# Products of zeros between the transposes of a recurrent stage

## The chip, the cores and the metric

The kernel runs on one core of one Trainium2 chip. Its metric is the device time of one execution in microseconds. Before the change three runs took 1701.95, 1700.95 and 1701.09 us, a median of 1701.09.

The engines are named as in the profile: PE is TensorE (PEld its weight loads), DVE is VectorE, ACT is ScalarE, POOL is GpSimd, SP is the engine that issues the large transfers.

## What is computed

A sequence of up to 50 items for each of B = 1024 users is turned into a spike rate, and each rate is multiplied with the whole table of N = 100001 embeddings of 128 numbers:

```
emb = emb_table.at[0].set(0.0)
e = emb[seq]
prefix = jnp.cumsum(e, axis=1)
denom = jnp.minimum(t_idx[None, :], lengths[:, None]).astype(e.dtype)
uF = prefix / denom[:, :, None]
mean = uF.mean(axis=0)
var = uF.var(axis=0)
y = (uF - mean) * lax.rsqrt(var + BN_EPS) * gamma + beta
...
def step(v, x):
    v = v + (x - v) / TAU
    spike = atan_spike(v - V_TH)
    v = v - lax.stop_gradient(spike) * V_TH
    return (v, spike)
...
uF_out = spikes.mean(axis=0)
scores = uF_out @ emb.T
```

The result has 1024 x 100001 numbers, 409.6 MB.

## The kernel before, in words

The work has two stages. The first walks through the T = 50 steps of the sequence, with the 128 features on the partitions and the 1024 users along the free dimension, in two halves of 512 (one bank of PSUM each). The second multiplies the spike counts with the table, chunk by chunk, and stores the scores. The order of each engine's instructions is the order of the program, nothing is moved by a scheduler; waits are put in where a buffer or a value is needed.

A step t of the first stage (lines 270 to 346) goes as follows.

- POOL gathers the rows of step t + 1 from the table (`gather`, line 185): eight indirect transfers of 128 rows each into one of three buffers `e`. A buffer is free again when the transposes of its earlier step have read it.
- PE transposes the eight blocks of `e` and adds each onto the running sum in PSUM, `pre[0]` or `pre[1]` (line 282). Each of the eight waits for its own gather.
- DVE divides each half by the count of items (line 291, into `uF`) and takes its statistics (line 292). It needs the four transposes of that half.
- PE then adds the correction of the next step to `pre` (`correct`, line 242): it takes away what table row 0 has added, by a product over 50 rows.
- DVE merges the statistics (line 296), ACT takes the root (line 300) and shifts `uF` (line 303), DVE finds the spikes of the step before (`spike`, line 262).
- PE adds those spikes to the counts (`counted`, line 252): a bf16 product with the identity, 512 columns, one for each half, into two more banks of PSUM, `count[0]` and `count[1]`.
- DVE ends the inverse root (lines 314 to 320), ACT makes the input (line 328), DVE the membrane voltage (lines 336, 331).
- In steps 42, 44 and 46 a piece of the table is prepared for the second stage as well: eight transposes on PE (line 101), a copy on ACT (line 130), a subtraction on DVE (line 134).

On PE the order is therefore: transposes of step t, corrections of step t + 1, counts of step t - 1, transposes of step t + 1.

The first seven chunks of the table are fetched at the start of the program; the next are fetched in the second stage, in which each of the counts is multiplied with two parts of the table (`product`, line 146) and the result is scaled out of PSUM by DVE (line 409) and ACT (line 411) and stored.

Of the kernel before, what the change touches and what calls it, by code (L numbers as in the profile page):

```python
# [13 lines left out]
BF16 = mybir.dt.bfloat16  # L14
# [6 lines left out]
P = 128  # L21
# [6 lines left out]
BANK = 512  # L28
# [3 lines left out]
def rec_kernel(  # L32
# [9 lines left out]
    nc = tc.nc  # L42
    B, T = seq.shape
# [92 lines left out]
    def prepare(c, q, pt):  # L136
        turned(c, q, pt)
        upper(c, q, pt)
        lower(c, q, pt)
# [18 lines left out]
    with ExitStack() as ph:  # L158
        row0p = ph.enter_context(tc.tile_pool(name="rows0", bufs=1))
        once = ph.enter_context(tc.tile_pool(name="once", bufs=1))  # L160
# [21 lines left out]
        def gather(t):  # L182
            es[t] = gp.tile([P, B], F32, tag="e", name=f"e_{t}")
            for n in range(NB):
                nc.gpsimd.indirect_dma_start(  # L185
                    out=es[t][:, n * P : (n + 1) * P],
                    out_offset=None,
                    in_=table,
                    in_offset=bass.IndirectOffsetOnAxis(ap=idx[:, n, t : t + 1].bitcast(U32), axis=0),
                )  # L190
# [41 lines left out]
        count = [accp.tile([P, BANK], F32, tag=f"count{h}", name=f"count{h}") for h in range(B // BANK)]  # L232

        def only(t):

            l = sp.tile([T, D], F32, tag="l", name=f"l_{t}")
            nc.scalar.activation(l, r0n, AF.Copy, scale=ident[:T, t : t + 1])
            return l

        def correct(t, l):  # L240
            for h in range(B // BANK):
                nc.tensor.matmul(  # L242
                    pre[h],
                    lhsT=l,
                    rhs=zT[:, h * BANK : (h + 1) * BANK],
                    start=t == 0,
                    stop=False,
                    skip_group_check=True,
                )

        def counted(t, s, h):
            nc.tensor.matmul(
                count[h],
                lhsT=ident_h,
                rhs=s[:, h * BANK : (h + 1) * BANK],
                start=t == 0,
                stop=t == T - 1,
                skip_group_check=True,
            )

        def spike(s, v, cs):
            nc.vector.tensor_single_scalar(s[:, cs], v[:, cs], V_TH, ALU.is_ge)  # L262

# [6 lines left out]
        for t in range(T):  # L270
            last = t == T - 1
            if t + 1 < T:
                gather(t + 1)
            e = es.pop(t)
            if last:
                spike(s, v, whole)
                nc.vector.tensor_tensor(negv, s, v, ALU.subtract)
            uF = up.tile([P, B], F32, tag="uF", name=f"uF_{t}")
            bs = sp.tile([P, B // BANK, 6], F32, tag="bs", name=f"bs_{t}")
            for h, cs in enumerate(halves):  # L280
                for k in range(0, BANK, P):
                    nc.tensor.matmul(  # L282
                        pre[h][:, k : k + P],
                        lhsT=e[:, h * BANK + k : h * BANK + k + P],
                        rhs=ident,
                        start=False,
                        stop=last,
                        is_transpose=True,
                        skip_group_check=True,
                    )  # L290
                nc.vector.scalar_tensor_tensor(uF[:, cs], rlen[:, cs], 1.0 / (t + 1), pre[h], ALU.max, ALU.mult)  # L291
                nc.vector.bn_stats(bs[:, h, :], uF[:, cs])  # L292
            if not last:
                correct(t + 1, l)
            mv = sp.tile([P, 2], F32, tag="mv", name=f"mv_{t}")
            nc.vector.bn_aggr(mv, bs.rearrange("p h s -> p (h s)"))  # L296


            r = sp.tile([P, 1], F32, tag="r", name=f"r_{t}")
            nc.scalar.activation(r, mv[:, 1:2], AF.Sqrt, bias=eps)  # L300
            nm = sp.tile([P, 1], F32, tag="nm", name=f"nm_{t}")
            nc.vector.tensor_scalar_mul(nm, mv[:, 0:1], -1.0)
            nc.scalar.activation(uF, uF, AF.Identity, bias=nm)
            ve = sp.tile([P, 1], F32, tag="ve", name=f"ve_{t}")
            nc.vector.tensor_scalar_add(ve, mv[:, 1:2], BN_EPS)


            if t:
                if not last:
                    spike(s, v, whole)  # L310
                for h in range(len(halves)):
                    counted(t - 1, s, h)

            nc.vector.reciprocal(r, r)
            q = sp.tile([P, 1], F32, tag="q", name=f"q_{t}")
            nc.vector.tensor_mul(q, r, r)
            nc.vector.scalar_tensor_tensor(q, q, -0.5, ve, ALU.mult, ALU.mult)
            nc.vector.scalar_tensor_tensor(r, q, 1.5, r, ALU.add, ALU.mult)
            a = sp.tile([P, 1], F32, tag="a", name=f"a_{t}")
            nc.vector.tensor_scalar(a, r, hgb[:, 0:1], None, ALU.mult)  # L320

            vt = vp.tile([P, B], F32, tag=f"v{t % 2}", name=f"v_{t}")
            st = lp.tile([P, B], BF16, tag="s", name=f"s_{t}")

            def x(cs):
                nc.scalar.activation(vt[:, cs], uF[:, cs], AF.Identity, bias=hgb[:, 1:2], scale=a)  # L328

            def step(cs):  # L330
                nc.vector.scalar_tensor_tensor(vt[:, cs], negv[:, cs], -0.5, vt[:, cs], ALU.mult, ALU.add)  # L331

            if not last:
                x(whole)
                if t:
                    nc.vector.tensor_tensor(negv, s, v, ALU.subtract)  # L336
                step(whole)
                v, s = vt, st
                if t + 2 < T:
                    l = only(t + 2)  # L340

                if T - 8 <= t < T - 2 and t % 2 == 0:
                    q = (t - T + 8) // 2
                    prepare(0, q, vp.tile([P, HALF], F32, tag="v1", name=f"pt_{q}"))
# [7 lines left out]
        for h, cs in enumerate(halves):  # L352
            step(cs)
            spike(st, vt, cs)
            if h == 0:
                counted(T - 1, st, 0)
                nc.scalar.copy(countA, count[0][:, :P])
# [84 lines left out]
```

## Time and profile before

| | us |
|---|---|
| median of 3 runs | 1701.09 |
| lowest, highest | 1700.95, 1701.95 |
| profiled execution, its own time | 1702.82 |
| its span, first to last instruction | 1701.1 |

| part of the span | PE busy | DVE busy | ACT busy | POOL busy | granted clock of PE | DMA share |
|---|---|---|---|---|---|---|
| 0 to 64 | 27.96 | 21.33 | 11.24 | 41.41 | 0.59 | 0.76 |
| 64 to 504 | 242.80 | 279.40 | 110.56 | 291.68 | 0.55 | 0.16 |
| 504 to 597 | 58.91 | 70.42 | 28.57 | 45.26 | 0.56 | 0.12 |
| 597 to 1701 | 876.69 | 576.76 | 481.06 | 0.00 | 0.93 | 0.98 |

The first three rows are the first stage: the start, in which the table's first chunks come in; the steps; and the last steps, in which the second stage is prepared. The fourth row is the second stage. All columns but the last two are microseconds. The granted clock is the share of the full TensorE clock that the throttle gave, the DMA share the mean busy share of the core's 16 DMA engines. A busy PE is not a PE at its peak: the records of its products overlap, and their ends are modelled. What ended a wait is inferred from semaphores; "remote" stands where no instruction of the profile is found for it.

### The profile page before, as it was taken

What the parts mean: (1) busy time and instruction counts of PE and PEld (TensorE: products, weight loads), DVE (VectorE), ACT (ScalarE), POOL (GpSimd) and SP (SyncE); (2) the same over time, 40 slices, a digit from 0 to 9 for tenths busy, and PEclk for the clock granted to TensorE, in tenths of its full rate; (3) what the DMA queues carried; (4) which work ended last, traced back from release to release, by engine and by line L of the source; (5) the groups of instructions that cost most, each with busy time, mean ns of one, the idle gap of its engine ahead of it and who ended that gap; (6) DMA issues with size and microseconds to landing.
All of it is one profiled execution on the core that took longest, in us unless ns stands there. A gap on an engine that the chain in (4) does not pass through costs nothing.

```text
span 1701.1 us, 13009 instructions
## 1 busy us (share of the span) xinstructions
PE 1206.4 (71%) x4621; PEld 844.5 (50%) x4634; DVE 947.9 (56%) x1257; ACT 631.4 (37%) x698; POOL 378.4 (22%) x406
## 2 busy tenths in 40 slices
PE   5445554565456597877777887777777778888886
PEld 2122222222223376666555665655655556666664
DVE  3556665676567774554455555554454555556553
ACT  2222222222222354444444444444444444445442
POOL 7666666666666200000000000000000000000000
PEclk6555555555555598999999999899999999999998
DMA  9211111111111089999999999999999999999998
GB/s 348 95 45 45 47 48 47 43 48 48 47 44 47 22 344 408 424 422 409 410 401 407 401 407 402 405 410 411 402 402 406 401 400 397 425 416 415 419 415 346
DMA packets 58329, 488.12 MB, mean 287 GB/s; under 512 B 12485, under 2 KB 13208, under 8 KB 33688
## 3 DMA queue, kind: packets, MB, share of 16 engines
q1 hardware_dynamic: 45464, 461.06, 66.1%
q0 software_dynamic: 12800, 26.24, 5.3%
q8 instruction: 36, 0.59, 0.1%
q14 instruction: 29, 0.24, 0.0%
HBM read 77.65 MB, written 409.60 MB: 286 GB/s over the span
## 4 chain that ended last, share of the span: by engine, by line
DMA 43%; DVE 22%; PE 15%; another core or an unknown queue 10%; ACT 6%; issue 3%; POOL 0%; SPq 0%; ACTq 0%; DVEq 0%; POOLq 0%
DMA scores<-o 42%; PE po L146 14%; ACT o L411 4%; DVE bs L292 4%; DVE uF L291 4%; DVE v L331 3%; DVE s L262 3%; DVE negv L336 2%; DVE o L409 2%; ACT v L328 1%; DMA e<-in_L_rec_emb_table,idx 1%; DVE mv L296 1%; PE pt L101 1%; DVE a L320 1%
## 5 line engine op out<-in xcount | busy, mean ns | idle before, releaser
L409 DVE TENSOR_SCALAR o<-po 128x1024 f32<-128x1024 f32 x390 | 463.1, 1220 | 473.9 <-DMA scores<-o 351.9
L411 ACT ACTIVATE o<-po 128x1024 f32<-128x1024 f32 (+1 forms) x390 | 385.1, 1018 | 573.0 <-DMA scores<-o 376.1
L146 PE MATMUL po<-hi,countC 128*128 128x512 f32 x784 | 343.1, 438 | 155.0 <-ACT o L411 154.9
L185 POOL DMA_INDIRECT e<-in_L_rec_emb_table,idx x400 | 377.7, 944 | 190.4 <-issue 109.4
L242 PE MATMUL pre<-zT,l 50*128 50x512 f32 x200 | 183.8, 1065 | 233.1 <-DVE uF L291 221.6
L146 PE MATMUL po<-lo,countC 128*128 128x512 f32 x784 | 327.0, 418 | 0.0
L146 PEld LDWEIGHTS po<-hi,countC 128*128 128x128 f32 x784 | 162.1, 207 | 215.2 <-ACT o L411 182.4
L146 PE MATMUL po<-hi,countB 128*128 128x512 f32 x588 | 234.7, 399 | 22.1 <-ACT o L411 22.1
L146 PE MATMUL po<-lo,countB 128*128 128x512 f32 x588 | 229.6, 391 | 0.0
L242 PEld LDWEIGHTS pre<-zT,l 50*128 50x128 f32 x200 | 54.0, 301 | 305.7 <-issue 265.5
L146 PEld LDWEIGHTS po<-lo,countC 128*128 128x128 f32 x784 | 162.3, 207 | 31.9
L291 DVE SCALAR_TENSOR_TENSOR uF<-rlen,pre 128x512 f32<-128x512 f32 x100 | 67.8, 678 | 185.3 <-remote 172.0
L300 ACT ACTIVATE r<-mv,eps 128x1 f32<-128x1 f32 x50 | 14.7, 295 | 384.0 <-DVE mv L296 280.7
L134 DVE TENSOR_TENSOR lo<-pt,hi 128x1024 fp32r<-128x1024 f32 x98 | 117.3, 1217 | 50.6 <-ACT hi L130 45.8
L101 PE MATMUL pt<-ident,rows 128*128 128x128 f32 x782 | 107.5, 282 | 44.6 <-ACT o L411 39.3
L146 PEld LDWEIGHTS po<-hi,countB 128*128 128x128 f32 x588 | 110.9, 189 | 54.3 <-ACT o L411 32.2
L101 PEld LDWEIGHTS pt<-ident,rows 128*128 128x128 f32 x782 | 90.3, 144 | 73.1 <-ACT o L411 58.1
L146 PEld LDWEIGHTS po<-lo,countB 128*128 128x128 f32 x588 | 111.1, 189 | 21.8
L130 ACT CAST hi<-pt 128x1024 fp32r<-128x1024 f32 x98 | 99.0, 1011 | 45.3 <-PE pt L101 40.3
L282 PE MATMUL pre<-ident,e 128*128 128x128 f32 x400 | 99.5, 423 | 14.0 <-DMA e<-in_L_rec_emb_table,idx 10.4
L282 PEld LDWEIGHTS pre<-ident,e 128*128 128x128 f32 x400 | 86.2, 228 | 39.4 <-issue 23.9
L328 ACT ACTIVATE v<-uF,hgb,a 128x1024 f32<-128x1024 f32 (+1 forms) x51 | 60.8, 1192 | 49.1 <-DVE a L320 24.8
(58 smaller groups left out, 701.6 us busy)
## 6 DMA issues: line engine op xcount, KB each, us to landing
scores<-o SPq DMA_DIRECT2D x190, 2048.0 KB
rows<-in_L_rec_emb_table SPq DMA_DIRECT2D x24, 2048.0 KB
scores<-o SPq DMA_DIRECT2D x8, 848.5 KB
e<-in_L_rec_emb_table,idx POOLq DMA_INDIRECT x400
scores<-o SPq DMA_DIRECT2D x2, 1024.0 KB
scores<-o SPq DMA_DIRECT2D x3, 512.0 KB
scores<-o SPq DMA_DIRECT2D x2, 256.0 KB
rows<-in_L_rec_emb_table SPq DMA_DIRECT2D x1, 512.0 KB
```

The lines of the kernel that those rows point to most:

```text
L101: nc.tensor.transpose(pt[:, k0 : k0 + kw], rows[c][:kw, q * KQ + k0 // P, :], ident[:kw, :kw])
L130: nc.scalar.copy(vh, vp)
L134: nc.vector.tensor_tensor(vl, vp, vh.bitcast(F32), ALU.subtract)
L146: nc.tensor.matmul(po[:, :kw], lhsT=counts[n], rhs=part[:, k0 : k0 + kw], start=j == 0, stop=j == 1,)
L185: nc.gpsimd.indirect_dma_start(out=es[t][:, n * P : (n + 1) * P], out_offset=None, in_=table, in_offset=bass.IndirectOffsetOnAxis(ap=idx[: ...
L242: nc.tensor.matmul(pre[h], lhsT=l, rhs=zT[:, h * BANK : (h + 1) * BANK], start=t == 0, stop=False, skip_group_check=True,)
L282: nc.tensor.matmul(pre[h][:, k : k + P], lhsT=e[:, h * BANK + k : h * BANK + k + P], rhs=ident, start=False, stop=last, is_transpose=True, ...
L291: nc.vector.scalar_tensor_tensor(uF[:, cs], rlen[:, cs], 1.0 / (t + 1), pre[h], ALU.max, ALU.mult)
L292: nc.vector.bn_stats(bs[:, h, :], uF[:, cs])
L328: nc.scalar.activation(vt[:, cs], uF[:, cs], AF.Identity, bias=hgb[:, 1:2], scale=a)
L409: nc.vector.tensor_scalar_mul(o[:, h0 : h0 + hw], po[:, :hw], 1.0 / T)
L411: nc.scalar.mul(o[:, h0 : h0 + hw], po[:, :hw], 1.0 / T)
```

## The change

A tile of zeros is made once on DVE. From step 2 on, PE adds three products of that tile with itself to the counts behind each of a step's transposes but the last. A product has 128 rows, 128 columns of weights and 512 moving columns in bf16, as one of the counts has; the three go to `count[0]`, `count[1]` and `count[0]` again. They add zero, so the counts keep their values. There are seven such places in a step, 21 products in each of the steps 2 to 49, and 1008 in all; each comes with a load of its weights. Nothing else moves: the order on the other engines is the same, but for the one clearing on DVE ahead of the first step.

```diff
+        zero = once.tile([P, BANK], BF16, tag="zero", name="zero")
+        nc.vector.memset(zero, 0.0)
+
+        def idle():
+            for h in (0, 1, 0):
+                nc.tensor.matmul(
+                    count[h],
+                    lhsT=zero[:, :P],
+                    rhs=zero,
+                    start=False,
+                    stop=False,
+                    skip_group_check=True,
+                )
...
                         is_transpose=True,
                         skip_group_check=True,
                     )
+                    if 1 < t and h * BANK + k + P < B:
+                        idle()
                 nc.vector.scalar_tensor_tensor(uF[:, cs], rlen[:, cs], 1.0 / (t + 1), pre[h], ALU.max, ALU.mult)
```

## The prediction

> **What bounds the kernel now.** I read the slices first, then busy time by stage, then one stretch of the first stage in order of time, then the granted clock around that stretch.
>
> ```profile
> PE   5445554565456597877777887777777778888886
> POOL 7666666666666200000000000000000000000000
> PEclk6555555555555598999999999899999999999998
> DMA  9211111111111089999999999999999999999998
> ```
>
> A slice is 42.5 us. Thirteen of them are the first stage: POOL gathers, TensorE is granted half its clock, the DMA engines are nearly idle. After 597 us the stage of the products follows, with the DMA engines at 0.98, and nothing of the change reaches into it. So the change is worth what it does before 597 us. Busy time of the engines in stretches that run from one restart of POOL's gathers to the next (columns PE, PEld, DVE, ACT, POOL, clock, DMA share, GB/s):
>
> ```profile
> 4.08:60.69 56.61, 25.44 (x56) 11.15 (x56) 17.75 (x40) 8.62 (x12) 38.02 (x41) 0.57 0.82 306
> 60.69:94.72 34.03, 16.05 (x39) 7.97 (x40) 20.67 (x44) 8.61 (x12) 22.64 (x24) 0.55 0.16 47
> 197.31:231.46 34.15, 19.05 (x41) 8.96 (x42) 21.88 (x46) 8.61 (x12) 22.64 (x24) 0.55 0.16 46
> 504.22:527.04 22.82, 14.56 (x36) 7.75 (x38) 16.59 (x34) 6.75 (x9) 15.09 (x17) 0.57 0.16 46
> 527.04:549.75 22.71, 15.88 (x38) 7.64 (x37) 16.40 (x33) 6.75 (x9) 15.09 (x16) 0.58 0.16 47
> ```
>
> The reader is to see one number in all five. 40 gathers in 56.61 us, 24 in 34.03 and 34.15, 16 in 22.82 and 22.71 are each 1.415 to 1.426 us a gather, in runs of five, three and two steps, under heavy DMA traffic (306 GB/s) and light. POOL issues a gather every 1.25 us, though, as the order of time shows:
>
> ```profile
> 217.28 0.94 POOL L185 DMA_INDIRECT e<-in_L_rec_emb_table,idx  x1 [0.30 <-PE pre L242]
> 217.73 1.92 PE L282 MATMUL pre<-ident,e 128*128 128x128 f32 x8
> 218.53 0.94 POOL L185 DMA_INDIRECT e<-in_L_rec_emb_table,idx  x1 [0.31 <-issue]
> ...
> 226.02 0.94 POOL L185 DMA_INDIRECT e<-in_L_rec_emb_table,idx  x1 [0.30 <-issue]
> 231.09 0.69 DVE L291 SCALAR_TENSOR_TENSOR uF<-rlen,pre 128x512 f32<-128x512 f32 x1 [10.81 <-remote]
> 231.46 0.94 POOL L185 DMA_INDIRECT e<-in_L_rec_emb_table,idx  x1 [4.50 <-remote]
> 231.93 3.75 PE L242 MATMUL pre<-zT,l 50*128 50x512 f32 x4 [12.28 <-DVE uF L291]
> ```
>
> Transposes start at 202.29, 210.01 and 217.73, a step every 7.72 us. VectorE gets the third step's sum not at 219.7, where the transposes end, but at 231.09, 4.1 us after POOL has run out of buffers; POOL waits for the same thing. So three steps take 34.1 us, 11.4 each. I read this as a pace of 1.42 us a gather that POOL's rows do not show and that comes out as a stall in every third step. The trace has no row for the cause ("remote"), so this is a reading and not a sight. The clock in windows of 3.4 us (the two numbers ahead of DMA's GB/s are clock and DMA share):
>
> ```profile
> 213.15:216.55 3.40, 3.33 (x4) 1.12 (x4) 3.30 (x7) 1.16 (x2) 2.49 (x4) 0.50 0.18 49
> 216.56:219.96 3.40, 3.08 (x11) 1.87 (x10) 3.05 (x8) 1.70 (x3) 2.48 (x4) 0.50 0.16 46
> 219.98:223.37 3.39, 0.00 (x0) 0.00 (x0) 0.30 (x1) 0.00 (x0) 2.63 (x3) 1.00 0.21 60
> 650.06:653.45 3.39, 1.09 (x5) 0.56 (x3) 0.00 (x0) 0.00 (x0) 0.00 (x0) 1.00 1.05 443
> 735.39:738.78 3.39, 1.72 (x11) 1.19 (x10) 1.56 (x2) 1.58 (x2) 0.00 (x0) 1.00 1.06 423
> 738.80:742.20 3.40, 3.40 (x20) 2.86 (x19) 2.00 (x2) 1.35 (x2) 0.00 (x0) 1.00 1.01 424
> ```
>
> A window filled by the 50-row corrections (213 to 216) does not raise the clock. One three quarters full of counts and transposes does, and the idle one behind it takes it back. At full clock a window half busy keeps it (735, next still 1.00), a nearly empty one (650) loses it.
>
> [...] here 216.56 to 219.96 holds little but 0.85 us of counts and 1.7 us of transposes and raises it[...]. [...] The trace has two counts in 1.03 us with 0.609 for the last, 0.42 a product, and 0.23 for the stage-two products at full clock.
>
> **The change part by part.** One clearing of a tile on VectorE, before the first step: nothing. In steps 2 to 49, behind seven of the eight transposes, three products of 512 columns: 21 a step, 1008 in all. They wait for nothing, but the transposes behind them wait for them, so a step's *transpose phase* grows. It was 8 x 0.213 (1.91 us with 0.42 for the last) and becomes 8 x 0.213 + 21 x 0.427 = 10.7 us at half clock, and 8 x 0.107 + 21 x 0.216 = 5.4 at full (0.107 as half of 0.213; the stage-two transposes take 1.06 for eight). Behind the last transpose hang VectorE's second half (L291), the correction, the count, the next phase, and POOL, whose next gathers write the buffer that the transposes read. From L291's second half to the count is 3.18 us (213.72 to 216.90), from count to transposes 0.83 (half) or 0.43. With 0.3 for the hand-over the loop is 5.4 + 0.3 + 3.2 + 0.4 = 9.3 us at full clock, 15.0 at half, for 7.7 now. VectorE's own work hides under it.
>
> One group of three steps, in us behind the stalled L291 (231.09 is zero):
> - Before: gathers from 0.4, count 4.5, transposes 5.3 to 7.3.
> - After, first phase: PE has sat idle, so the clock is half at 5.3. The first window three quarters busy ends 2.6 to 6.0 us behind the count at 4.5; I take 4.3, so the clock rises at 8.8. By then 3.5 us of 10.7 are done, the other 7.2 take 3.6: end 12.4 (11.5 to 13.2).
> - POOL's second eight want to start at 10.4 and need that phase's end: 12.7. At 1.42 the first eight are through at 11.8, so the gathers lose 12.7 - 11.8, and the rest of the hand-over: 1.3 us (0 to 2.1).
> - Second phase 16.3 to 21.7, third 25.6 to 31.0. If the clock falls in the pauses of 3.5 us between (corrections and count, a window that the trace leaves open), each ends 1.7 later, the third at 34.7. Gathers 9 to 24 take 16 x 1.42 = 22.7 from 12.7: 35.4. So the third phase stays hidden, barely, and a group costs 1.3 us.
>
> Sum: 13 groups (60.69 to 504.22) x 1.3 = 17. Three pairs with eight transposes more in the second step, whose phase starts only near 20.5 and ends near 26 against 22.7 now: 3 x 3.4 = 10. Steps 48 and 49, which no gather paces, 2 x 2.5 (1.6 at full clock, 3.3 mixed) = 5. Step 2 lies under the stall of 35 to 56 us: nothing. Together +32 us on the profiled execution's 1702.8, so 1735; the median of the runs shown is 1.7 lower, so **1733**.
>
> **The rivals.**
> - *The stall goes* (faster). If the pile of "remote" waits comes from eight transposes in one burst and not from the gathers, spreading them removes it. Then POOL's 1.25 us sets the pace: 400 x 1.25 + 4 = 504 for the end of the gathers, at 569.4 now: -65, +5 for the tail, so 1643; with the clock going up and down, steps of 10.5 to 11 and some 1665 to 1685. For it: no data is missing at 219. Against it: the same 1.42 in five stretches, with transposes spread by waits in the first of them. It decides if a stretch of 24 gathers falls under 34 us.
> - *Hidden*. The clock rises at once in each group, the 1.3 and 3.4 vanish, and the tail is left: +3, 1704 on the median at most.
> - *The clock does not rise* (the change doesn't do what it says): products of zeros count as little as 50 rows do. The loop is 15.0: from step 3's transposes at 64.4, 46 loops end at 754 against 583.9 for step 49's now, +170: 1873. For it: the unraised window of 213. Against: those rows are 50 of 128, these 128. With the clock up half the time, 1780 to 1830.
>
> **How the numbers follow.** Main case 0.62, within 1710 to 1770 (groups from 0.3 to 3 us by the bounds of the first phase and of falling clocks). Clock low 0.10, of which 0.04 under 1800. Hidden 0.12. Stall gone 0.16, of which a quarter is above 1685. The range 1685 to 1800 holds 0.62 + 0.04 + 0.12 + 0.04 = 0.82; the main case's own is 1710 to 1770. Two tenths of a per cent are 3.4 us, about what these runs can tell. Faster takes the stall's 0.16 and a little of Hidden, 0.17; within takes most of Hidden, 0.11; slower 0.72.
>
> **What would show it.** Granted clock in 64 to 504 us: some 0.8 if the step is right, 0.55 if zeros do not count, 0.95 if Hidden is. Transpose phases of 7 us in a group's first step and of 5.4 to 7 in the others. 24 gathers in 35 to 36 us, with POOL waiting for PE ahead of the second eight. L291's "remote" wait shrinks from 10.8 us to a few, because the third phase fills it: it is not time gained. It would be wrong if those waits vanished and the stretch fell toward 30 us, or if the clock fell inside every phase, which takes groups over 38.

## The result and the profile after

The changed kernel takes 1730.20 us (median of 4 runs, 1729.96 to 1730.57), the kernel before 1701.28 (4 runs). The ratio is 1.017, 95% interval 1.0152 to 1.0187. The profiled execution took 1730.02 us, its span 1728.2. The page's slices, 43.2 us each:

```profile
PE   6587887878887887888878777777777788888886
POOL 7566666666665400000000000000000000000000
PEclk7688888888887789999999998998999999999998
DMA  9211111111111139999999999999999999999998
```

The change does what it says: the granted clock is at 0.6 to 0.8 in the first stage, and PE is busy there. Yet the gathers (POOL) reach a little farther to the right. The windows of the stages (PE, PEld, DVE, ACT and POOL busy, clock, DMA share, GB/s):

```profile
64.00:504.00 440.00, 362.07 (x1285) 167.22 (x1310) 277.00 (x563) 107.68 (x151) 282.49 (x299) 0.83 0.16 45
504.00:597.00 93.00, 75.08 (x274) 36.75 (x277) 56.88 (x111) 23.12 (x31) 54.89 (x59) 0.80 0.15 42
597.00:1728.00 1131.00, 901.25 (x3976) 701.42 (x3976) 598.68 (x539) 489.68 (x502) 0.00 (x0) 0.93 0.96 395
```

The clock of 64 to 504 went from 0.55 to 0.83, PE's busy time there from 242.8 to 362.1 us, and POOL did less in it (282 for 292). The merged statistics of step 49, the end of the first stage, come at 621.67 us instead of 591.69, 30.0 later; what follows is 2.9 us shorter. So all of the loss lies in the first stage: 4.7 us up to step 3, 10.0 in steps 4 to 41 (11.76 us each, 11.50 before), 15.2 in the last eight.

Who made POOL and VectorE wait (total us, times, longest), first before, then after:

```profile
DVE uF L291 <- remote: 172.0, 19, 20.6
POOL e L185 <- remote: 64.3, 16, 4.5
POOL e L185 <- PE pre L242: 7.9, 5, 6.7
```

```profile
DVE uF L309 <- PE pre L298: 87.9, 47, 3.5
DVE uF L309 <- remote: 64.1, 8, 24.3
POOL e L185 <- PE pre L298: 45.7, 20, 6.4
POOL e L185 <- PE pre L242: 31.4, 17, 2.0
POOL e L185 <- remote: 26.8, 8, 6.4
```

(Line 309 is line 291 of the kernel before, 298 is 282.) VectorE's "remote" wait fell by 108 us, and no time was gained by it: its waits ahead of this line, whatever ended them, went from 185 to 209 us together, and POOL now waits 104 us instead of 72, 77 of them for PE, in 37 waits and not once in a group. The regular groups of three steps are gone. Times of a typical stretch, read from the starts of the transposes and of the statistics in the trace:

| step | transpose phase, first to last start | mean clock in it | last transpose to second half's statistics | step |
|---|---|---|---|---|
| 16 | 5.30 | 1.00 | 3.47 | 11.56 |
| 17 | 6.95 | 0.76 | 1.52 | 11.65 |
| 18 | 6.25 | 0.85 | 2.25 | 11.68 |
| 19 | 5.29 | 1.00 | 1.89 | 9.98 |
| 20 | 5.30 | 1.00 | 6.01 | 14.10 |
| 21 | 7.07 | 0.75 | 1.03 | 11.41 |

Two things are in it. In some steps part of the phase runs at half clock, and in some VectorE gets its sum late (1.03 us is what it needs). The experiments take them apart.

### The profile page after: what moved, and what is told of

Same layout as the page of the kernel before. It is cut to its first block, busy times and chain, and to the rows that moved or that the text cites. A ratio compares the mean times of both kernels' runs of the same rounds, so it can differ in the third digit from the quotient of the medians.

```text
span 1728.2 us, 15006 instructions
## 1 busy us (share of the span) xinstructions
PE 1368.8 (79%) x5609; PEld 918.9 (53%) x5642; DVE 953.8 (55%) x1258; ACT 631.7 (37%) x698; POOL 379.0 (22%) x406
## 4 chain that ended last, share of the span: by engine, by line
DMA 42%; PE 35%; DVE 11%; ACT 5%; another core or an unknown queue 4%; issue 2%; POOL 1%; SPq 0%; ACTq 0%; DVEq 0%; POOLq 0%
DMA scores<-o 41%; PE po L146 14%; PE count L268 13%; ACT o L429 5%; PE pre L298 4%; DVE s L278 3%; DVE uF L309 2%; DVE bs L310 2%; PE pre L242 2%; PE count L252 2%; DVE o L427 2%; POOL e L185 1%; PE pt L101 1%; DVE v L349 1%
## 5 line engine op out<-in xcount | busy, mean ns | idle before, releaser
L268 PE MATMUL count<-zero 128*128 128x512 bf16 x988 | 305.3, 433 | 1.3 <-issue 0.4
L242 PE MATMUL pre<-zT,l 50*128 50x512 f32 x200 | 124.7, 726 | 65.6 <-DVE uF L309 65.5
L268 PEld LDWEIGHTS <-zero 128*128 128x128 bf16 x1008 | 111.4, 111 | 96.7 <-issue 40.0
L298 PE MATMUL pre<-ident,e 128*128 128x128 f32 x400 | 124.1, 312 | 10.2 <-DMA e<-in_L_rec_emb_table,idx 7.1
L298 PEld LDWEIGHTS pre<-ident,e 128*128 128x128 f32 x400 | 65.0, 163 | 74.3 <-issue 30.3
```

The source lines that it names most:

```text
L242: nc.tensor.matmul(pre[h], lhsT=l, rhs=zT[:, h * BANK : (h + 1) * BANK], start=t == 0, stop=False, skip_group_check=True,)
L268: nc.tensor.matmul(count[h], lhsT=zero[:, :P], rhs=zero, start=False, stop=False, skip_group_check=True,)
L298: nc.tensor.matmul(pre[h][:, k : k + P], lhsT=e[:, h * BANK + k : h * BANK + k + P], rhs=ident, start=False, stop=last, is_transpose=True, ...
```

## Experiments

The runs fell on five chips, and these differ: beside our runs the kernel before took 1702.5 and 1699.6 us on two of them, 1619.1, 1618.8 and 1619.1 on three. The chip of the prediction is of the first kind, *with the stall*. Every run is set against the kernel before on its own chip. The runs under 1, 2 and 3 are one execution each.

Theories at the start, with the letters that expectations use: A, the reading on record, that the gathers have a pace of 1.42 us each which shows as a stall; B, that the stall comes from PE's side, by the pile of transposes; and, from the third run on, "late rows", that the gathered rows come later than recorded, against C, that the completions of PE's work reach the other engines late while POOL gathers.

**1. No gathers (chip with the stall).** SP copies other rows of the table as they lie, so that the sums are those of other rows; once in the kernel before and once in the changed kernel.

```diff
-                nc.gpsimd.indirect_dma_start(
+                nc.sync.dma_start(
...
-                    out_offset=None,
-                    in_=table,
-                    in_offset=bass.IndirectOffsetOnAxis(ap=idx[:, n, t : t + 1].bitcast(U32), axis=0),
+                    in_=table[(t * NB + n) * P : (t * NB + n + 1) * P, :],
```

> The kernel before, with the indirect gathers replaced by plain transfers of table rows from the SP queue (other rows are summed, so the scores differ; bytes and transposes are the same). Theory A, the gathers carry a pace of 1.42 us each and that is the stall: no stall in any step, 7.72 us a step from about 60 us on, last merged statistics near 435 instead of 592, whole about 1545 us. Theory B, the stall belongs to PE and comes with every 24 transposes: still 34 us for three steps, about 1700 us.

> The kernel after with the same replacement (other rows are summed). It shows PE's loop with the added products alone. Theory A: no stalls and no waits of POOL, steps of 9.3 us where the clock is full and up to 11 where it falls in the pauses, mean 10 to 10.5, last merged statistics near 62 + 47 x 10.3 = 546, whole about 1655 us; so the added products cost some 110 us against plain_rows, where the gathers hid all but 29. Theory B: about 1730, as after.

Measured 1545.71 us without products: from step 2 to step 42 the steps take 7.72 us (one takes 8.00), the clock is mostly half (0.829 in the mean of the whole execution), no sum is late. With products 1662.28: steps of 9.12, 10.81 and 10.79 us in turn, 10.24 in the mean. So the stall is there with POOL's gathers and not without them (1702.52 and 1545.71 us; B falls), and the products alone cost 117 us where the gathers hide nothing. The loop of 9.12 us at full clock is the 9.3 of the prediction. But the clock does not stay full in all steps.

**2. Gathers that nobody reads (chip with the stall).** The transposes of the kernel before read one fixed tile; the gathers are issued as ever. (The lines that load this tile once, at the start, are left out here.)

```diff
...
-            e = es.pop(t)
+            e = fixed
+            es.pop(t)
```

> The kernel before, with all gathers issued as before but every step's transposes reading one tile of fixed rows (other rows are summed); nothing on PE depends on a gather any more, and POOL never waits for PE. If the third step is late because its rows are late: no stalls, 7.72 us a step, and the gathers end at their own pace, 4 + 400 x 1.42 = 572 us under theory A, 504 us if 1.25 us is their true pace; the second stage's first buffers wait for them, so about 1680 us or 1615 us. If PE's completions are reported late while gathers pile up (theory C): VectorE still waits about 11 us or more for sums whose transposes are recorded as done.

Measured 1963.09 us, a step of 39.20 us as long as POOL gathers and of 7.72 once it has ended. A step of it in order of time, the gathers left out (they go on at 1.25 us):

```profile
126.76 1.91 PE L285 MATMUL pre<-ident,fixed 128*128 128x128 f32 x8 [0.22 <-issue]
...
150.87 0.69 DVE L294 SCALAR_TENSOR_TENSOR uF<-rlen,pre 128x512 f32<-128x512 f32 x1 [21.49 <-remote]
...
162.06 0.69 DVE L294 SCALAR_TENSOR_TENSOR uF<-rlen,pre 128x512 f32<-128x512 f32 x1 [9.78 <-remote]
```

Eight transposes are recorded from 126.76 to 128.67. VectorE, which waits for nothing else, gets the first four at 150.87 and the other four at 162.06. Late rows are excluded: these rows lay there from the start. What is measured fits C: POOL, which never waits for PE here, issues a gather every 1.25 us without a pause, and every step has such waits, 39.20 us apart. In the other direction nothing is late: VectorE's spikes end at 165.11 in the same step, and PE's counts, which wait for them, start at 165.16. So a PE row's end in this trace can't be read as the time at which VectorE gets the result: 23 us lie between for the first four and 33 for the others. I call that delay the hold.

With half of the transposes (blocks 0, 2, 4, 6; sums of the others left out), once on a chip without the stall and once on one with it:

```diff
-                for k in range(0, BANK, P):
+                for k in range(0, BANK, 2 * P):
```

> As the kernel whose transposes read one fixed tile, but with four transposes in a step instead of eight (blocks 0, 2, 4 and 6; the other blocks get no sum). The gathers still run and nobody reads them. There a step took 39.2 us, of which 11.2 lay between the reports of the first and of the second four transposes. If each PE instruction is held for the same time, 2.8 us a transpose, the step falls to 39.2 - 4 x 2.8 = 28.0 us and the whole run to about 1963 minus what 14 such steps save, which the longer reach of fewer steps gives: some 1880. If the hold is one fixed wait per step, it stays at 39.2 us.

> The kernel with four transposes of one fixed tile in each step (the other blocks get no sum) once more, for a chip with the stall. Without the stall 1605 us. With it a step of 28.0 us if each transpose is held for 2.8 us, of 39.2 if the hold is one fixed wait in a step.

On the chip without the stall 1605.66 us, steps of 7.72 us beside running gathers and no "remote" wait. On the one with it 1908.99, and steps of 28.00 us, as a hold of 2.8 us for each transpose predicts:

```profile
151.74 0.69 DVE L294 SCALAR_TENSOR_TENSOR uF<-rlen,pre 128x512 f32<-128x512 f32 x1 [4.88 <-remote]
173.44 0.69 DVE L294 SCALAR_TENSOR_TENSOR uF<-rlen,pre 128x512 f32<-128x512 f32 x1 [15.20 <-remote]
179.74 0.69 DVE L294 SCALAR_TENSOR_TENSOR uF<-rlen,pre 128x512 f32<-128x512 f32 x1 [4.88 <-remote]
```

Line 294 at 151.74 and 179.74 is the same half of two steps, 28.00 apart. Four transposes fewer took 11.2 us off the step, 2.8 each. Both steps leave 16.8 us for the rest, more than twice a whole step without the hold (7.72), so transposes alone do not account for it; I take it that the corrections and counts are held as well. (The sum of "some 1880" was wrong: only six more steps fit beside the gathers, which saves 6 x 7.72 = 46 us behind them; the gathers end 5.3 us earlier, too, and the last statistics come 51.8 us earlier of the 54 measured.) Whether PE itself works that slowly or only reports late, the trace doesn't tell; nor what makes two chips do it and three not.

A rival stands in the same traces and was not tested. While POOL gathers on a chip with the stall, the profile has few records of semaphore updates, from which it infers what ended a wait. Between 200 and 300 us the two kernels with the fixed tile have 143 and 142 of them there, about one in 0.70 us. VectorE's late sums lie on steps of 0.7 us as well: 11.19 us apart in the first kernel, 21.70 and 6.30 in the second, 16, 31 and 9 times 0.70. The second of these kernels has 1565 on the chip without the stall, some 121 for a step of 7.72 us where the stalled chip has some 40 for one of 28.00. The first kernel of run 1 has 2027, on a chip with the stall but without gathers from POOL. So the hold could belong to the recording of an execution and not to the work of the chip; each time of these experiments comes with a recorded span and clock, so no run separates the two. And where such records are few, the name of what ended a wait is less sure than the wait.

**3. Products over 32 rows (chip with the stall).** The changed kernel with its added products over 32 of the 128 rows.

```diff
-                    lhsT=zero[:, :P],
-                    rhs=zero,
+                    lhsT=zero[:32, :P],
+                    rhs=zero[:32, :],
```

> The kernel after with the added products over 32 rows instead of 128; PE streams the same 512 columns. If the clock gate weighs a product by its rows: granted clock about 0.55 in the steps, loop 15.0 us, about 1873 us. If any product counts alike: clock 0.83 and 1730 us.

Measured 1999.48 us, a step of 17.44 but for those in which the table is prepared. In order of time:

```profile
258.04 1.46 PE L268 MATMUL count<-zero 32*128 32x512 bf16 x3
259.42 0.47 PE L298 MATMUL pre<-ident,e 128*128 128x128 f32 x1
259.83 1.46 PE L268 MATMUL count<-zero 32*128 32x512 bf16 x3
```

A place takes 1.79 us, the phase 12.50. Products last 0.62 us and transposes 0.47 in the mean; at half clock in the kernel before, counts last 0.62 and transposes 0.42. PE is busy for 397.3 of the 400 us from 100 to 500, and by these durations the clock does not rise: products over 32 rows did not raise it here, where those over 128 gave 0.83. The phase is 1.8 us longer than the 10.7 worked out for half clock at 128 rows, so the time was under-priced. Over 128 rows a place takes 1.50 us at half clock, as priced (run 5, between the transposes at 227.69 and 229.19); why 32 rows take 1.79 is not shown. (This execution has no record of the clock changing in its first stage; the durations decide.)

**4. One and two products in each place, and two buffers.**

```diff
-            for h in (0, 1, 0):
+            for h in (0,):
```

and `(0, 1)` for two; the third kernel is the one before with `bufs=2` for the gathered rows. These ran on a chip without the stall.

> The change with one product of zeros in each of the seven places instead of three. At half clock a transpose phase is 1.91 + 7 x 0.43 = 4.9 us and the loop 4.9 + 0.3 + 3.2 + 0.8 = 9.2 us, under the 11.4 us that a step takes beside the gathers. If the gathers have a pace of their own (1.42 us each), the products lie under it and only the last two steps show: 1702 to 1706 us, groups of three kept, 34.1 us each. If PE's completions are what is late, drained one by one at some 0.7 us per PE instruction while the gathers run, the products lengthen the stall by up to 14 x 0.7 us for each group: up to 1838 us; if the spreading of the transposes relieves it, under 1690.

> The change with two products in each place. Loop 7.8 us at full clock, 12.2 at half. With the clock up half the time some 10 us, still under 11.4: 1703 to 1715 us if the gathers have a pace of 1.42 of their own. With the clock down 12.2 x 46 steps ends at 1738. As for the kernel with one product, late completions could make it longer or, by way of POOL waiting in each step, shorter.

> The kernel before with two buffers for the gathered rows instead of three, no products. If each gather takes 1.42 us of its own, nothing changes: 1701 us, now in stretches of two steps, 22.7 us. If completions of PE are held while POOL issues gathers without a pause, POOL runs into its wait sooner and the hold is cut short: stretches of two steps of 20 to 22.7 us, 1640 to 1701. If the hold grows only behind some number of gathers, 16 may be too few for it and the stall vanishes: 10.0 us a step, 1640.

Measured beside 1619.06: 1619.48 with one product (ratio 1.0007, interval 0.9999 to 1.0016), 1619.96 with two (1.0007, 0.9999 to 1.0016), 1619.12 with two buffers (1.0001, 0.9992 to 1.001). There POOL has no pause over 0.3 us. The waits of the kernel with two buffers:

```profile
PE pre L282 <- DMA e<-in_L_rec_emb_table,idx: 118.9, 178, 1.1
POOL e L185 <- issue: 116.1, 381, 0.3
POOL e L185 <- PE pre L282: 2.4, 8, 0.3
```

PE waits for rows, 178 times, POOL never more than 0.3 us, and a step is eight gathers at 1.25 us, 10.0. One or two products, loops under 10.0, disappear below that; two were not run on a chip with the stall. The two-buffer run tells nothing of the stall, since there was none.

**5. The change on a chip without the stall.**

> The changed kernel once more, because the kernel before took 1701 us on one chip and 1619 on another, where its gathers run at 1.25 us without a stall. On a chip with the stall: 1730 us beside 1701, a ratio of 1.017. On a chip without it the gathers need 10.0 us a step and the products, which alone made steps of 9.13 to 10.81 us, 10.24 in the mean, set the pace: (10.24 - 10.0) x 46 = 11 us, and the last eight steps, where a step of the kernel with two products already takes 11.6 to 13.5 us, 8 to 15 more: 1635 to 1645 beside 1619, a ratio near 1.013.

Measured 1640.70 us beside 1618.83, ratio 1.014 (1.0123 to 1.0157). So the loss doesn't need the stall. The steps are 9.12, 10.81, 10.78 us in turn, as without gathers, each sum at its time. In the traces of the kernel before and of the changed kernel every recorded stretch of one granted clock but the last is 3.41 us or a whole multiple of it. The windows of 3.41 us over one such turn:

```profile
219.59:223.00 3.41, 3.41 (x19) 1.91 (x17) 2.14 (x4) 0.00 (x0) 2.79 (x3) 1.00 0.22 58
223.00:226.42 3.42, 2.20 (x7) 0.73 (x6) 3.21 (x10) 1.33 (x2) 2.51 (x3) 1.00 0.20 54
226.42:229.84 3.42, 3.42 (x12) 1.52 (x10) 2.63 (x4) 1.53 (x2) 2.50 (x4) 0.50 0.18 47
229.84:233.25 3.41, 3.36 (x18) 1.98 (x18) 1.38 (x2) 0.00 (x0) 2.55 (x3) 1.00 0.23 58
```

The second window has PE busy for 2.20 us and still costs the next one its clock: 1.67 us of it are 50-row corrections. A step behind it runs 3.4 us at half clock, 1.7 us lost. Steps of 10.24 in the mean exceed POOL's 10.0.

These corrections count for less than their time, but not for nothing, as two windows show, the first from this run, the second from the kernel with one product:

```profile
212.77:216.18 3.41, 2.77 (x9) 0.97 (x8) 2.41 (x6) 0.82 (x2) 2.50 (x4) 1.00 0.14 38
92.47:95.88 3.41, 1.97 (x10) 0.74 (x8) 1.38 (x2) 0.00 (x0) 2.50 (x4) 1.00 0.20 49
```

The first has 1.98 us of corrections and 0.79 of work over 128 rows, and the next window keeps the full clock. The second has 1.88 us over 128 rows and 0.09 of corrections, and the next window is at half. If corrections counted for nothing, one would expect the other way round. An estimate of their weight, from the 694 windows at half clock between 64 and 640 us in all these kernels but the one of run 3: with 0.4 of a correction's time counted, a sum of some 2.6 us in a window tells those that raise the clock from the others with 6 errors; with none of it counted there are 14, with all of it 136, each at its own best limit. In the traces of before and after alone it is 2, 3 and 37 for 198 such windows, and for the 140 at full clock, by which of them the clock falls, 1, 5 and 21. The weight is a rough one: the two windows above, taken alone, ask for more than 0.58 (1.88 less 0.79, over 1.98 less 0.09).

**6. One product on a chip with the stall.**

> The kernel with one product in each place once more, for a chip with the stall. If the kernel before takes 1619 us there: 1619 again. If it takes 1701: with the stall kept in stretches of 34.1 us and the products under it 1702 to 1706; if each product lengthens the hold (14 PE instructions a step at 0.7 us) up to 1838; if POOL's wait in each step takes the stall's place, as in the changed kernel, 1705 to 1730.

Measured 1703.99 us beside 1699.60, ratio 1.0018 (1.0008 to 1.0029). The hold is not longer, so it is not 0.7 us for every PE instruction, which had up to 1838 us on record; the products lie under the stall; the groups, however, are mostly of two steps now:

```profile
173.34 0.94 POOL L185 DMA_INDIRECT e<-in_L_rec_emb_table,idx  x1 [2.94 <-remote]
195.93 0.94 POOL L185 DMA_INDIRECT e<-in_L_rec_emb_table,idx  x1 [2.93 <-remote]
218.48 0.94 POOL L185 DMA_INDIRECT e<-in_L_rec_emb_table,idx  x1 [2.89 <-remote]
```

Sixteen gathers in 22.59 and 22.55 us, 1.41 each: a pause of 2.9 us for 16 gathers where the kernel before has 4.5 for 24. So the mean pace of 1.42 keeps through another pattern, though a gather's row on POOL lasts 0.94 us as ever.

**7. The pause filled (chip without the stall).** If the fallen windows are the cost, products in the pause ahead of the counts must take it away. Five more go there, from step 2 on:

```diff
             if not last:
                 correct(t + 1, l)
+                if 1 < t:
+                    idle((0, 1, 0, 1, 0))
```

> The changed kernel with five more products of zeros behind the corrections of each step, in the pause before the counts. In the changed kernel the clock falls for one window of 3.41 us in two of three steps, behind windows that hold little but 50-row corrections; at full clock five products are 1.08 us of the 1.22 us that PE waits there. If the fallen windows are what makes its steps 10.81 us instead of 9.12, the clock stays up and every step can be 9.1 us: on a chip without the stall the products then lie under the gathers' 10.0 us, 1620 to 1628 us beside 1619 instead of 1641; on a chip with it 1700 to 1712 beside 1701 instead of 1730. If the loop itself is what counts, the five products make it longer: 1645 to 1655, or 1735 to 1745.

Measured 1620.51 us beside 1619.12, ratio 1.0008 (1.0002 to 1.0015). PE does more, and the loss of 1.4% is a loss of 0.08%, 20 us less. Four windows in a row:

```profile
216.20:219.62 3.42, 3.23 (x10) 1.20 (x11) 3.14 (x8) 1.34 (x2) 2.50 (x4) 1.00 0.22 58
219.62:223.03 3.41, 3.41 (x20) 2.00 (x19) 3.09 (x7) 1.53 (x2) 2.80 (x3) 1.00 0.22 58
223.03:226.44 3.41, 3.03 (x15) 1.35 (x13) 1.25 (x3) 0.00 (x0) 2.50 (x4) 1.00 0.19 52
226.44:229.86 3.42, 3.39 (x12) 1.12 (x12) 3.21 (x10) 1.33 (x2) 2.50 (x4) 1.00 0.20 49
```

The clock is full from 37 to 443 us without a break, and a step is POOL's 10.0 us again. In the chain of work that ended last, PE has 38% of the span in run 5 and 19% here, POOL 1% and 16%.

It wasn't tried on a chip with the stall. It doesn't beat the kernel before; nothing here does.

## Why the prediction came out

The total was right, 1730 for 1733, as were most prices. The picture inside was partly wrong.

- *Prices at full clock: right.* The phase is 5.30 us (5.4 predicted), the loop 9.12 (9.3). At half clock no run held the change's own products for a whole phase; single places took 1.50 us there, and seven of them with one transpose are the 10.7. The 0.216 for a product at full clock had no row of before behind it, which has 0.23 in the second stage; in the trace of after the added products start 0.216 us apart at full clock and 0.427 at half, and a transpose takes 0.109 and 0.213. The loop of 15.0 stays untested.
- *The clock rises: right.* 0.83 (0.8) for 0.55 before, with zeros over 128 rows. That the few rows of the corrections do not raise the clock was read from one window; 69 windows of the kernels of that estimate in run 5 hold over 3.0 us of them, and none of the windows behind them is at full clock; the trace of before has 13, and none raised it. They do count a little (run 5). That transposes count was read from a window that held counts as well; one of before with nothing but transposes, 520.35 to 523.74 with PE busy for 2.96 us, raised it too: the next, to 527.14, is at 1.00. The window of 650 with PE busy for 1.09 us did lose it: the next, 653.46 to 656.85, is at 0.50.
- *The clock between phases: a term that was undersized.* "If the clock falls in the pauses of 3.5 us" stood in the prediction as a bound, and the sum used phases of 5.4 for the second and third step. It does fall, in two steps of three, at 1.7 us each as said. Run 7 shows that this is what the change costs on a chip without the stall: with the clock kept up 1.4 us are left of 22.
- *The groups of three: wrong.* There are none left. POOL waits for PE ahead of most steps, not only of the second eight, and the steps lie at 11.4 to 12.1 us, with pairs of 10.0 and 14.1 between. The term's size was near, and that is luck: 13 x 1.3 = 17 was predicted for POOL's wait in each group, the steps up to 41 lost 14.75 with no group left, 4.7 of it already by step 3, where nothing was expected. The four stretches of 24 gathers that I took lie at 34.9 to 36.7 us (35 to 36 predicted).
- *The last steps: right in sum.* 10 + 5 = 15 predicted, 15.2 lost. The 2.9 us that the second stage gave back were not foreseen; run 7 gained there as well (its step 49 ends 6.2 us later than with two buffers, its total is 1.4 later). Why was not tried.
- *The nature of the stall: half right, and open.* As a mean, 1.41 to 1.42 us a gather holds in both patterns, groups of three and of two, and it was right to refuse the gain: "no time gained" is what VectorE's smaller wait meant. What the reading missed is that sums of PE reach VectorE late while POOL gathers, 23 and 33 us behind the rows' ends in run 2. The trace of before showed both faces, rows on POOL at 1.25 and a "remote" wait of 10.81 us that ended at 231.09, 11.4 us behind the transposes. A pace of the gathers behind POOL is not refuted: in the first kernel of run 2 nobody reads the rows, and POOL still starts its second 200 gathers 1.40 us apart in the mean, on the chip without the stall 1.25. Which of the two makes the other is not shown.
- *The rivals.* "Stall goes" fell here: the stall lessened as a wait and the kernel lost. "Hidden" is close to what one product does on a chip with the stall (1.0018), and on the others what one or two do; with three only run 7's filled pause reaches it. "Clock does not rise" is run 3.
- *Slips without weight.* The first stage takes fourteen slices, not thirteen, and the DMA engines are nearly idle only from the second on. A third phase that ends at 31.0 and comes twice 1.7 us later ends at 34.4, not 34.7.

Left open: on the chip with the stall the changed kernel's steps of 11.76 us are 1.5 above the 10.24 of run 5, just as the 11.50 of before are above 10.0. The stall thus kept its price of 1.5 us a step beside the slower loop, instead of absorbing it. Runs 5 and 7 explain the loss where there is no hold; that the same fallen windows make it here is likely, since they are in the trace, but not shown. The loss is spread alike: the last eight steps have 15.2 of 29.9 us here, and 12.7 of 24.6 in run 5 (set against the kernel with two buffers, whose trace stands for the kernel before on such a chip).

## What to carry to other kernels

Here work added to warm PE kept the clock up only where each window of the loop held enough of it: behind one with 2.20 us of PE, 1.67 of them 50-row corrections, the clock fell (run 5); with five more products the windows held 3.03 to 3.41 us, and it stayed (run 7). So look for the emptiest 3.4 us, count products over few rows there for less than their time (some 0.4 here, a rough estimate), and fill that one first. Before pricing such work, ask what the clock buys: here a loop of 7.72 us at half clock was already below the gathers' 10.0, so a warm PE could gain nothing. A "remote" wait behind a PE row that has ended may be for PE all the same, as the one of 21.49 us in run 2: a kernel in which nothing else is waited for tells. And a stall read on one chip may not be on the next.

## What the runs showed of the hardware

- The same program, the kernel before, takes 1618.8 to 1619.1 us on three chips and 1699.6 to 1702.5 on two. Where it takes longer, VectorE gets PE's sums late beside POOL's gathers (23 us behind the rows' ends for the first four transposes of run 2, 33 for the others), and the profile has few records of semaphore updates (142 in 100 us, 1565 for the same kernel on a chip without the stall). Whether the delay is there without recording is open.
- With gathers running and no pause, a step took 39.20 us there with eight transposes and 28.00 with four, 2.8 us a transpose; late sums lay 11.19, 21.70 and 6.30 us apart in those two kernels, multiples of 0.7. On a chip without the stall the step with four took 7.72.
- In the traces of before and after, on the chip with the stall, the packets of a gather (the first forty gathers apart) start 1.6 to 2.9 us behind its start on POOL. With nobody reading the rows POOL issued at 1.25 us at first and, on a chip with the stall, from about the 200th gather at 1.40 in the mean; its rows between 478 and 538 us last 0.94 to 1.80 us there, where they lasted 0.94 to 0.96 between 119 and 165. What slows them is not shown.
- Products over 32 rows kept PE busy for 397.3 of 400 us and did not raise the clock; the change's products over 128 rows brought it from 0.55 to 0.83. Corrections over 50 rows count for some 0.4 of their time (a rough estimate, run 5). A window with 2.96 us of transposes and nothing else raised it from 0.50 to 1.00.
